# A four-layer graph network on one core: the block order of hop 2 and of layer 3, kept blocks counted from resident masks, and row 0 of each mask through GpSimd's queue

## The chip, the cores and the metric

The kernel runs on one core of a Trainium2 chip. The metric is the device time of one execution in microseconds (us). An execution recorded by the hardware profiler has a span (first to last instruction) besides.

## The reference, cut to what matters

Input: 3327 nodes with 64 features, `x`, and a sparse weighted matrix `adj` (3327 x 3327). Four residual layers follow each other, each with a layer norm. Layers 0 and 1 come before the part that is changed. Layer 2 has two hops, and layer 3 weights the neighbours of a node by their rank, counted from the last one, and keeps at most 100:

```python
# layer 2
for k in range(2):
    agg = adj @ x
    x = jnp.tanh(jnp.concatenate([agg, x], axis=1) @ W[k])
# layer 3
support = input @ weight
mask = (adj != 0)
rank = jnp.cumsum(mask, axis=1)
deg = rank[:, -1:]
k = jnp.minimum(deg, 100.0)
pos = rank - (deg - k)
w = mask * jnp.where(pos > 0, 0.5 ** (k - pos), 0.0)
out = w @ support + bias
# after each layer
x = layernorm(x + layer(x))
```

## The kernel before, in words

**Tiling.** The matrix is passed in transposed and padded to 3328. It is cut into 26 blocks of 128 rows (the neighbours j) by 3328 columns (the nodes i); a block in f32 is 1664 KB. The 3328 columns are two halves of 1664, and a half is four chunks of 416. `slot` gives the place of a block's features.

**Buffers.** Seven blocks stay in SBUF: 25 to 22 (`kept`, loaded at the start) and 20, 21, 19 (tile `late`). The rest is streamed through five buffers: four in pool `strm` (loads named `at_l`) and one in pool `more` (`bt_l`). `block` (L214) issues a load on SyncE's queue; the load waits until the last user of its buffer is done.

**Layer 2.** Each hop (loop `k`, L490) adds block after block into PSUM: `add` (L512) is two matmuls (the two halves of the columns, 64 output rows each) for a chunk, sixteen for a block, on line 515. `top` and `bottom` (L500, L505) bring in the weights, `chunk_end` (L615) adds the blocks in `end` and does the tanh. Hop 1 takes the four blocks loaded early, then kept blocks with three streamed ones after each. Its last five streamed blocks (14 to 18) are still in their buffers when hop 2 starts and are hop 2's `ready`.

**Counts for layer 3.** Layer 3 needs for each block the number of neighbours that come after it. `t_masks` (L439) makes 0/1 masks in bf16 of a block on VectorE, one for each half, into the buffers `tm` and `over`; `t_counts` (L448) adds them up on TensorE (line 452, eight matmuls a block) into `t_ps`. In hop 1 this starts with the ninth block of the order, for kept and streamed blocks alike; kept blocks not counted by the end of the loop (25, 21, 19) are counted around the hop's end (L624 to L631). The first seven streamed blocks (0 to 6) are counted in hop 2. When all 26 are counted, `t_out` (L459) writes them to `t_rows` in DRAM by GpSimd's queue.

**Resident masks.** In hop 2, `both_masks` (L360) writes a whole block's mask (128 x 3328 bf16, VectorE) into `over` or into a half of the memory of a kept block that hop 2 has used already (`slots_of`). The dictionary `place` says after which step of the order which block is masked into which place. In this kernel the masks of the seven kept blocks and of the streamed blocks 17 and 18 end up resident: nine of the 26.

**Layer 3.** `steps` lists 52 pairs (half, block). Those whose mask isn't resident, 34 of them, are loaded again as half blocks of 832 KB (`load`, tile `ah`, four buffers) and masked by `masks(q)` (six buffers, L369). Row 0 of each mask is not the mask's first row but the count of the blocks after it: it is fetched from `t_rows` by a small DMA. In this kernel `masks` puts the step on a list, and `first_row` (L351), called at the head of the next step, issues the DMA on ScalarE's queue. For a resident mask GpSimd's queue does it once for both halves (L614).

For each step q and each of two column groups c: `count` (L643) multiplies a triangle with the mask into PSUM (line 646), `read` (L651) turns the counts into weights (ScalarE, or VectorE for c = 1 in odd steps), and `products` (L843) multiplies them with the features. The high parts are multiplied at once (line 851), the low parts once in seven steps (line 868, 28 matmuls). The loop at L1021 holds the order: `read(·, q)`, one entry of `with_step`, at most one `masks` of the list `to_mask` (as long as fewer than six mask buffers are held), `products(q - 3, ·)` and `count(·, q + 1)` through `advance`. PSUM for the counts is one tile for each c, so the count of step q + 1 waits for the read of step q. The list `with_step` splits the features of the parts B, C, E of the blocks in steps 3 to 9: a copy on ScalarE, then a subtraction on GpSimd (`other_parts`, L779). The entry of step 9 also calls `first_rows` (L876), sixteen small DMAs on GpSimd's queue into `sf`, which `first_products` (L889) multiplies. `firsts_weighted`, in step 6, is three operations of VectorE.

**What sets the order.** In these layers the order on TensorE and GpSimd, and on VectorE and ScalarE, is that of the program text (`manual_schedule`). A queue runs its entries one after the other: what stands behind a waiting instruction waits too. The DMAs of SyncE's queue are issued as their buffers come free.

Of the kernel before, what the change touches and what calls it, by code (L numbers as in the profile page):

```python
# [21 lines left out]
NB = 26  # L22
# [3 lines left out]
HALF = NP // 2  # L26
NBH = NB // 2
# [17 lines left out]
FIRST_T = 8  # L45
BATCH_T = 2
# [35 lines left out]
def kernel(  # L82
# [11 lines left out]
    nc = tc.nc  # L94
# [42 lines left out]
    kept = {}  # L137
# [67 lines left out]
    for h in range(2):  # L205
        rows, last = slice(h * D, (h + 1) * D), slice((h + 1) * D - 1, (h + 1) * D)
# [106 lines left out]
    def layers(ctx, x2, x3, begun_here, kept, ready, ahead_ctx, strm):  # L313
# [9 lines left out]
        over = carry.tile([P, NP], BF16, name="over")  # L323
        t_rows = dram.tile([NB + 1, NP], BF16, name="t_rows")
# [7 lines left out]
        in_order.enter_context(  # L332
            tc.manual_schedule(engines={mybir.EngineType.PE, mybir.EngineType.Pool})
        )
        steps = [(h, jb) for h in range(2) for jb in range(NB - 1, -1, -1)]
        mask, ws = {}, {}

        ahead, to_load = {}, []
# [7 lines left out]
                    ahead[q], adjT[jb * P : (jb + 1) * P, h * HALF : (h + 1) * HALF]  # L346
                )

        no_row = []

        def first_row(keep):  # L351
            while len(no_row) > keep:
                q = no_row.pop(0)
                h, jb = steps[q]
                half = slice(h * HALF, (h + 1) * HALF)
                nc.scalar.dma_start(mask[q][:1, :], t_rows[jb + 1 : jb + 2, half])

        resident = {}

        def both_masks(jb, at):  # L360

            nc.vector.tensor_scalar(at, blocks[jb], 0.0, None, ALU.not_equal)  # L362
            resident[jb] = at

        def slots_of(jb):
            at = kept[jb].bitcast(BF16)
            return at[:, :NP], at[:, NP:]

        def masks(q):  # L369
            h, jb = steps[q]  # L370
            mask[q] = l3m.tile([P, HALF], BF16, tag="mask", name=f"mask_{h}_{jb}")
            nc.vector.tensor_scalar(mask[q], ahead.pop(q), 0.0, None, ALU.not_equal)  # L372
            no_row.append(q)
            load()

        groups = fours
# [52 lines left out]

            return rows.rearrange("b (h c k) -> c b h k", h=2, c=CPH)  # L430

        t_done, t_made, t_begun, t_ps = set(), [], set(), []

        def halves_of(t):
            return [t[:, h * HALF : (h + 1) * HALF] for h in range(2)]
# [3 lines left out]
        def t_masks(jb):  # L439

            t_done.add(jb)
            for h, of in enumerate(halves_of(blocks[jb])):
                m = t_at.pop(0)
                t_at.append(m)
                nc.vector.tensor_scalar(m, of, 0.0, None, ALU.not_equal)  # L445
                t_made.append((jb, h, m))
# [36 lines left out]
        with tc.tile_pool(  # L483
# [6 lines left out]
            for k in range(2):  # L490
# [36 lines left out]
                order = list(ready)  # L527
                if k:
                    end = [jb for jb in kept if jb not in soon]
                    for i, jb in enumerate(soon):  # L530
                        order.insert(2 * i + 1, jb)
                    order += others
                    place = {
                        0: [(soon[0], over)],
                        1: list(zip(soon[1:3], slots_of(soon[0]))),
                        3: list(zip((soon[3], end[0]), slots_of(soon[1]))),
                        6: [(order[6], slots_of(soon[2])[0])],
                        7: list(zip(end[1:], slots_of(soon[3]))),
                        8: [(order[8], slots_of(soon[2])[1])],
                    }  # L540
# [45 lines left out]
                for i, jb in enumerate(order):  # L586
                    if jb not in blocks:
                        if len(seen) % (UNDER_WAY + MORE) < MORE :
                            blocks[jb] = held[jb] = block(more, jb, tag="bt", name=f"bt_l2_{k}_{jb}")
                        else:  # L590
                            blocks[jb] = block(strm, jb, tag="at", name=f"at_l2_{k}_{jb}")
                        seen[jb] = blocks[jb]
                    if i or not k:
                        for c in range(CPH):
                            add(c, jb)
                    if jb not in t_done and (k or i >= FIRST_T):
                        t_masks(jb)
                        if len(t_made) == len(t_at) or len(t_done) == NB:
                            t_counts()
                    if k:  # L600
                        for b, at in place.get(i, ()):
                            both_masks(b, at)
                    if k == 0 and begun_here:

                        if i == 8:
                            for c in range(CPH):
                                bottom(c)

                            warm_t = small.tile([P, 1], F32, tag="warm", name="warm_t")
                            nc.scalar.activation(warm_t, hT[:, :1], AF.Tanh)  # L610
                    if k and i == 8 + len(t_left):
                        t_out()
                        for b, at in resident.items():
                            nc.gpsimd.dma_start(at[:1, :], t_rows[b + 1 : b + 2, :])  # L614
                def chunk_end(c):  # L615
                    for jb in end:
                        add(c, jb, jb == end[-1])
# [2 lines left out]
                if k:  # L620
                    break
                t_counts()
                t_left = [jb for jb in order if jb not in t_done and jb not in kept]
                last_t = [jb for jb in kept if jb not in t_done]  # L624
                for i, jb in enumerate(last_t):
                    t_masks(jb)
                    if i % BATCH_T == BATCH_T - 1 and jb != last_t[-1]:
                        t_counts()
                for c in range(CPH):
                    chunk_end(c)  # L630
                t_counts()  # L631

                last = sorted(list(seen)[-UNDER_WAY - MORE :], key=lambda jb: jb not in held)
                ready = {jb: seen[jb] for jb in last}
# [44 lines left out]
        more_ctx.close()  # L679
        l3m = ctx.enter_context(tc.tile_pool(name="l3m", bufs=MASKS, reuse_waits="tile"))  # L680
        m0 = first_masks()
        for q, (h, jb) in enumerate(steps):
            if jb in resident:
                mask[q] = resident[jb][:, h * HALF : (h + 1) * HALF]
# [157 lines left out]

        def products(q, c):  # L843
            h, jb = steps[q]
            first, last = jb == NB - 1, jb == 0
            if first:
                acc[h, c] = acc_tile(f"acc3_{h}_{c}")[:, :, :CW]

            def high(q, c):
                for e in range(2):  # L850
                    nc.tensor.matmul(  # L851
                        acc[h, c][:, e, :], s12[:, slot(jb)].rearrange("p t d -> p (t d)"),
                        ws[q, c][:, e, :], start=first, stop=last,
                    )
# [1181 lines left out]
```

## Time and profile before

| what | value |
|---|---|
| time, three runs | 559.77, 560.41, 561.75 us (median 560.41) |
| the profiled execution | 558.62 us; its span 556.9 us |
| TensorE clock granted | 0.987 |
| busy over the span | TensorE 91%, VectorE 73%, ScalarE 53%, GpSimd 41% |
| hop 1 of layer 2 | first matmul at 237.0 us, last block at 324 us |
| hop 2 | from 325 us to 423 us |
| layer 3, loop over 52 steps | from about 430 us to 543 us |

How it is read: a line of a timeline has the start, the length, the engine, the source line, what is written from what, how many instructions were merged, and in brackets the idle time ahead and what ended it. A line of waits has who waited, for whom, the total in us, how often, and the longest. A line of the DMA view ends with the size in KB and the median time from issue to landing. `PE` is TensorE, `DVE` VectorE, `ACT` ScalarE, `POOL` GpSimd, `SPq` SyncE's queue. The tile `cnt` on line 515 is the memory of hop sums, which layer 3 uses for its counts. `x2` and the like are numbers of instructions in a line.

### The profile page before, as it was taken

The numbers are of one execution on the slowest core, as the hardware profiler recorded it, in microseconds if no ns is written. First come the engines' busy times: TensorE is split into PE (matmuls) and PEld (weight loads), VectorE is DVE, ScalarE is ACT, GpSimd is POOL, SyncE is SP. The second block draws the span as 40 slices with busy tenths as digits, with TensorE's granted clock in tenths as the row PEclk, the third lists the DMA queues.
The fourth block names the chain that finished last, engine by engine and source line by source line (L and its number), as shares of the span: only waits on it lengthen the run. The fifth ranks groups of instructions, "written<-read, shape, count | busy, mean of one in ns | idle before, by whom it ended". The sixth has DMA issues, their size and how long they took to land. (4 is left out here: it accounts for less than half of the span.)

```text
span 556.9 us, 7703 instructions
## 1 busy us (share of the span) xinstructions
PE 509.1 (91%) x2865; PEld 209.5 (38%) x2865; DVE 404.1 (73%) x577; ACT 293.6 (53%) x345; POOL 229.6 (41%) x121
## 2 busy tenths in 40 slices
PE   8889999999999999999999899899788789989892
PEld 5522222222222223944333344333234344454442
DVE  6899999999999999898555616653027976456513
ACT  4899999999999996600000010000016756566541
POOL 4599999999999996000000000001410270000000
PEclk9999999999999999899999999999999999999997
DMA  8978776676777454999996007699961799907501
GB/s 298 346 227 291 238 241 225 213 241 203 234 241 226 142 217 152 376 423 425 425 427 257 1 0 261 245 416 421 386 232 44 242 390 402 388 1 233 231 1 36
DMA packets 34138, 139.20 MB, mean 250 GB/s; under 512 B 11199, under 2 KB 12977, under 8 KB 28971
## 3 DMA queue, kind: packets, MB, share of 16 engines
q1 hardware_dynamic: 30503, 137.29, 66.9%
q10 hardware_dynamic: 2404, 0.70, 0.6%
q0 software_dynamic: 1184, 0.63, 0.5%
q8 instruction: 24, 0.39, 0.3%
q14 instruction: 23, 0.19, 0.1%
HBM read 136.93 MB, written 1.04 MB: 248 GB/s over the span
## 5 line engine op out<-in xcount | busy, mean ns | idle before, releaser
L1251 POOL TENSOR_TENSOR sg<-sg,at 128x1664 f32<-128x1664 f32 x44 | 163.5, 3742 | 1.3 <-ACT sg L1239 1.2
L1279 ACT ACTIVATE pq<-pq,al,ga 128x832 f32<-128x832 f32 x104 | 104.7, 1012 | 10.9 <-DVE a L1278 10.9
L1266 PE MATMUL pq<-riT,ljT 64*128 64x416 f32 x416 | 100.8, 561 | 10.3 <-DVE v L1287 6.2
L1287 DVE SCALAR_TENSOR_TENSOR v<-pq,a 128x832 f32<-128x832 f32 x104 | 105.4, 1014 | 3.2 <-ACT pq L1279 2.2
L1278 DVE SCALAR_TENSOR_TENSOR a<-pq,sg 128x832 f32<-128x832 f32 x104 | 105.2, 1012 | 0.5 <-PE prep_fours L1357 0.4
L515 PE MATMUL cnt<-at_l,lj 128*64 128x416 f32 x496 | 91.4, 515 | 4.3 <-DMA at_l<-in_adjT 4.3
L1296 PE MATMUL acc<-v,xv 128*64 128x416 f32 x416 | 95.3, 537 | 0.0
L1239 ACT ACTIVATE sg<-lb,rb 128x1664 f32<-128x1664 f32 (+1 forms) x53 | 87.2, 1648 | 0.0
L618 ACT ACTIVATE x<-cnt 128x416 f32<-128x416 f32 x8 | 4.1, 517 | 155.8 <-PE cnt L515 155.8
L661 ACT ACTIVATE w<-cnt 128x832 int16<-128x832 f32 x79 | 65.9, 864 | 36.9 <-PE cnt L646 24.2
L464 POOL DMA_DIRECT2D t_rows<-tb x4 | 2.6, 711 | 146.7 <-DVE tb L462 146.7
L1266 PEld LDWEIGHTS pq<-riT,ljT 64*128 64x128 f32 x416 | 31.3, 184 | 83.7 <-DVE v L1287 82.9
L515 PEld LDWEIGHTS cnt<-at_l,lj 128*64 128x64 f32 x496 | 34.3, 137 | 55.7 <-issue 48.1
L851 PE MATMUL acc<-w,s 128*128 128x416 bf16 x208 | 52.4, 339 | 1.3 <-DVE sq L755 0.5
L1296 PEld LDWEIGHTS acc<-v,xv 128*64 128x64 f32 x416 | 20.6, 134 | 61.8 <-issue 58.0
L372 DVE TENSOR_SCALAR mask<-ah 128x1664 bf16<-128x1664 f32 x34 | 35.5, 1057 | 11.0 <-DMA ah<-in_adjT 6.5
L515 PE MATMUL cnt<-kept,lj 128*64 128x416 f32 x224 | 41.7, 515 | 0.4 <-DVE lj L503 0.4
L659 DVE TENSOR_SCALAR w<-cnt 128x832 int16<-128x832 f32 x25 | 25.5, 1020 | 20.3 <-PE cnt L646 20.3
L646 PE MATMUL cnt<-mask,tri 128*128 128x416 bf16 x136 | 35.0, 338 | 5.4 <-DVE w L659 2.8
L646 PEld LDWEIGHTS <-tri 128*128 128x128 bf16 x208 | 19.7, 97 | 36.3 <-issue 21.6
L1251 POOL TENSOR_TENSOR sg<-sg,kept 128x1664 f32<-128x1664 f32 (+1 forms) x10 | 30.0, 3019 | 0.0
L445 DVE TENSOR_SCALAR tm<-at_l 128x1664 bf16<-128x1664 f32 x16 | 15.7, 1023 | 16.8 <-PE t L452 16.8
(317 smaller groups left out, 468.5 us busy)
## 6 DMA issues: line engine op xcount, KB each, us to landing
at_l<-in_adjT SPq DMA_DIRECT2D x27, 1664.0 KB
at<-in_adjT SPq DMA_DIRECT2D x44, 832.0 KB
ah<-in_adjT SPq DMA_DIRECT2D x34, 832.0 KB
kept<-in_adjT SPq DMA_DIRECT2D x7, 1664.0 KB
bt_l<-in_adjT SPq DMA_DIRECT2D x6, 1664.0 KB
lb<-lf_rows SPq DMA_DIRECT2D x2, 384.0 KB
mask<-t_rows ACTq DMA_DIRECT2D x34, 3.2 KB
ljT<-ljT SPq DMA_DIRECT2D x4, 128.0 KB
```

What stands on the lines that cost most here:

```text
L372: nc.vector.tensor_scalar(mask[q], ahead.pop(q), 0.0, None, ALU.not_equal)
L515: nc.tensor.matmul(acc[c][h * D : (h + 1) * D, :], hw[:, slot(jb), :], blocks[jb][:, o : o + CW], start=c not in begun, stop=last, skip_gr ...
L646: nc.tensor.matmul(cnt[c][:, e, :], tri, mask[q][:, of], start=True, stop=True, skip_group_check=True,)
L661: nc.scalar.activation(w.bitcast(I16), cnt[c], AF.Relu)
L851: nc.tensor.matmul(acc[h, c][:, e, :], s12[:, slot(jb)].rearrange("p t d -> p (t d)"), ws[q, c][:, e, :], start=first, stop=last,)
L1239: nc.scalar.activation(sg[:, :, of], lbs[:, :, of], AF.Sigmoid, bias=rb[:, sl : sl + 1])
L1251: nc.gpsimd.tensor_tensor(sg[:, :, of], sg[:, :, of], at[:, :, of], ALU.mult)
L1266: nc.tensor.matmul(pq[:, h, :], ljT[h != jb // NBH][rows, of], riT[rows, ch * CW : (ch + 1) * CW], start=True, stop=True,)
L1278: stt(a_s[t], pqs[t], CUBIC_PLUS, us.pop(t), op0=ALU.add, op1=ALU.mult)
L1279: nc.scalar.activation(pqs[t], pqs[t], AF.Square, bias=al[:, one], scale=ga[:, one])
L1287: stt(w, pqs.pop(t), CUBIC_REST, a_s.pop(t), op0=ALU.add, op1=ALU.mult)
L1296: nc.tensor.matmul(accs[cp, ci][h * D : (h + 1) * D, :], xv[:, slot(jb), :], w[:, h, :], start=(jb == orders[cp][0]), stop=(jb == orders[c ...
```

## The change

- **Hop 1** counts only streamed blocks (from the ninth of the order on): 7 to 18. No kept block is counted there.
- **Hop 2** takes its order as 14, 15, 16, 17, 18 (what hop 1 left), then 25, 24, 23, 22, then the streamed blocks 0 to 13. Before, the kept blocks 25 to 22 stood between the first five.
- **Resident masks** are now of the seven kept blocks and of 12 and 13, the last two streamed ones. `both_masks` puts a kept block on the list of what is to be counted, and `t_counts` counts it from the resident mask in hop 2. `t_out` comes when all are counted; the rows of 12 and 13 are fetched after the loop.
- **Layer 3's steps** are mixed. For the first half: 25, 24, 23, 22, 10, 11, 7, 8, 20, 9, 4, 5, 21, 6, 17, 18, 0, 19, 1, 2, 3, 12, 14, 15, 16, 13; for the second: 10, 11, 25, 7, 8, 24, 9, 4, 23, 5, 6, 22, 17, 18, 20, 0, 1, 21, 2, 3, 19, 14, 15, 12, 16, 13. Before, a half ran from 25 down to 0, the resident nine first.
- **Row 0** of a loaded mask is fetched by GpSimd's queue, in `masks` itself.

```diff
-        steps = [(h, jb) for h in range(2) for jb in range(NB - 1, -1, -1)]
+        steps = []
...
-        def first_row(keep):
-            while len(no_row) > keep:
-                q = no_row.pop(0)
-                h, jb = steps[q]
-                half = slice(h * HALF, (h + 1) * HALF)
-                nc.scalar.dma_start(mask[q][:1, :], t_rows[jb + 1 : jb + 2, half])
...
             nc.vector.tensor_scalar(at, blocks[jb], 0.0, None, ALU.not_equal)
             resident[jb] = at
+            if jb not in t_done:
+                t_done.add(jb)
+                t_made.extend((jb, h, m) for h, m in enumerate(halves_of(at)))
...
             nc.vector.tensor_scalar(mask[q], ahead.pop(q), 0.0, None, ALU.not_equal)
-            no_row.append(q)
+            half = slice(h * HALF, (h + 1) * HALF)
+            nc.gpsimd.dma_start(mask[q][:1, :], t_rows[jb + 1 : jb + 2, half])
             load()
...
+        def rows_of(jbs):
+            for jb in jbs:
+                nc.gpsimd.dma_start(resident[jb][:1, :], t_rows[jb + 1 : jb + 2, :])
...
-                    for i, jb in enumerate(soon):
-                        order.insert(2 * i + 1, jb)
-                    order += others
+                    r = len(order)
+                    order += soon + others
                     place = {
-                        0: [(soon[0], over)],
-                        1: list(zip(soon[1:3], slots_of(soon[0]))),
-                        3: list(zip((soon[3], end[0]), slots_of(soon[1]))),
-                        6: [(order[6], slots_of(soon[2])[0])],
-                        7: list(zip(end[1:], slots_of(soon[3]))),
-                        8: [(order[8], slots_of(soon[2])[1])],
+                        1: [(soon[0], over)],
+                        r: list(zip(soon[1:3], slots_of(soon[0]))),
+                        r + 1: list(zip((soon[3], end[0]), slots_of(soon[1]))),
+                        r + 3: list(zip(end[1:], slots_of(soon[3]))),
                     }
+                    for i, at in zip((-2, -1), slots_of(soon[2])):
+                        place[len(order) + i] = [(order[i], at)]
...
-                    if jb not in t_done and (k or i >= FIRST_T):
+                    if k and len(t_made) > 2 * BATCH_T:
+                        t_counts()
+                    if jb not in t_done and jb not in kept and (k or i >= FIRST_T):
                         t_masks(jb)
-                        if len(t_made) == len(t_at) or len(t_done) == NB:
+                        if len(t_made) >= len(t_at):
                             t_counts()
...
-                    if k and i == 8 + len(t_left):
+                    if k and len(t_done) == NB and not t_ends:
+                        t_ends.append(i)
+                        t_counts()
                         t_out()
-                        for b, at in resident.items():
-                            nc.gpsimd.dma_start(at[:1, :], t_rows[b + 1 : b + 2, :])
+                        rows_of(resident)
+                if k:
+                    rows_of(order[-2:])
...
-                last_t = [jb for jb in kept if jb not in t_done]
-                for i, jb in enumerate(last_t):
-                    t_masks(jb)
-                    if i % BATCH_T == BATCH_T - 1 and jb != last_t[-1]:
-                        t_counts()
                 for c in range(CPH):
                     chunk_end(c)
-                t_counts()
...
+        here = list(resident)
+        rest = [jb for jb in range(NB) if jb not in resident]
+        rest.sort(key=lambda jb: next(i for i, g in enumerate((10, 7, 4, 0)) if jb % NBH >= g))
+        for h in range(2):
+            n = len(here) - (4 if h == 0 else 0)
+            mixed = here[:-n]
+            late_here = here[-n:]
+            for i, jb in enumerate(rest):
+                mixed.append(jb)
+                while late_here and (i + 1) * n >= (n - len(late_here) + 1) * len(rest):
+                    mixed.append(late_here.pop(0))
+            steps += [(h, jb) for jb in mixed]
...
-            first, last = jb == NB - 1, jb == 0
+            first, last = q % NB == 0, q % NB == NB - 1
...
-            if c and jb == 6:
+            if c and q % NB == NB - 4:
                 first_products(h)
...
-            first_row(1 if to_mask else 0)
```

More of the change, by code (lines that the diff above doesn't have):

```diff
@@ L347, in load @@
                 )
-        no_row = []
-        def first_row(keep):
-            while len(no_row) > keep:
-                q = no_row.pop(0)
-                h, jb = steps[q]
-                half = slice(h * HALF, (h + 1) * HALF)
-                nc.scalar.dma_start(mask[q][:1, :], t_rows[jb + 1 : jb + 2, half])
         resident = {}
@@ L430, in by_chunk @@
             return rows.rearrange("b (h c k) -> c b h k", h=2, c=CPH)
-        t_done, t_made, t_begun, t_ps = set(), [], set(), []
+        t_done, t_made, t_begun, t_ps, t_ends = set(), [], set(), [], []
+        def rows_of(jbs):
+            for jb in jbs:
+                nc.gpsimd.dma_start(resident[jb][:1, :], t_rows[jb + 1 : jb + 2, :])
         def halves_of(t):
@@ L622, in layers @@
                 t_counts()
-                t_left = [jb for jb in order if jb not in t_done and jb not in kept]
-                last_t = [jb for jb in kept if jb not in t_done]
-                for i, jb in enumerate(last_t):
-                    t_masks(jb)
-                    if i % BATCH_T == BATCH_T - 1 and jb != last_t[-1]:
-                        t_counts()
                 for c in range(CPH):
                     chunk_end(c)
-                t_counts()
                 last = sorted(list(seen)[-UNDER_WAY - MORE :], key=lambda jb: jb not in held)
```

## The prediction

> **What bounds the kernel now.** I read the timelines of TensorE, SyncE's queue, GpSimd and VectorE from 230 us on, then the waits and the DMA view. The change leaves everything before hop 1 of layer 2 (237 us) alone. Hop 1 is bound by TensorE. It has no gap until its last blocks are counted, which VectorE's masks hold up:
>
> ```profile
> 314.49 0.53 PE L452 MATMUL t<-over,upto 128*32 128x416 bf16 x8
> 315.62 0.36 PE L452 MATMUL t<-tm,upto 128*32 128x416 bf16 x4 [0.60 <-DVE tm L445]
> ...
> 318.43 0.36 PE L452 MATMUL t<-over,upto 128*32 128x416 bf16 x4 [0.57 <-DVE over L445]
> 318.72 5.81 PE L515 MATMUL cnt<-kept,lj 128*64 128x416 f32 x32
> 324.45 0.54 PE L452 MATMUL t<-tm,upto 128*32 128x416 bf16 x8
> ```
>
> From 314.94 to 318.72 TensorE does only two kept blocks' counts (3.8 us), and a third block costs 0.47 us at 324.45. Hop 2 then ends in a DMA limit, with gaps ahead of each block:
>
> ```profile
> 401.44 3.01 PE L515 MATMUL cnt<-at_l,lj 128*64 128x416 f32 x16 [1.24 <-DMA at_l<-in_adjT]
> 406.34 3.01 PE L515 MATMUL cnt<-at_l,lj 128*64 128x416 f32 x16 [1.89 <-DMA at_l<-in_adjT]
> ```
>
> SyncE's queue says when its last stretch of loads began: block 4 at 360.12, block 5 at 361.99, and from there the DMA engines are full until 402.
>
> ```profile
> 360.12 0.33 SPq L216 DMA_DIRECT2D at_l<-in_adjT  x1
> ```
>
> Layer 3 (430 to 543 us) is a loop in which a mask, its count, its read and its product follow each other. Its waits from 422 us on:
>
> ```profile
> ACT w L661 <- DVE mask L372: 11.9, 7, 2.8
> DVE w L659 <- PE cnt L646: 20.3, 15, 5.1
> ...
> DVE mask L372 <- DMA ah<-in_adjT: 6.5, 5, 2.4
> ```
>
> VectorE waits for a load; its reads, in line behind, come late; and ScalarE, whose queue issues row 0, waits for the mask. VectorE's reads (every second step) are 3.16 us apart when nothing is late, 5.74 us with a batch of 28 L868 matmuls (2.58 us).
>
> GpSimd's queue is what the change loads. It holds this burst (L876 `first_rows`), beside VectorE's masks:
>
> ```profile
> 444.43 1.16 POOL L782 TENSOR_TENSOR s<-sq,s 128x512 bf16<-128x512 f32 x1 [5.12 <-ACT s L781]
> 445.53 1.04 POOL L883 DMA_DIRECT2D sf<-s  x1
> 446.56 0.54 POOL L887 DMA_DIRECT2D sf<-s  x1
> ...
> 452.32 1.30 POOL L883 DMA_DIRECT2D sf<-s  x1 [1.81 <-DMA sf<-s]
> ...
> 457.81 0.51 POOL L887 DMA_DIRECT2D sf<-s  x1
> ```
>
> ```profile
> m<-in_adjT POOLq DMA_DIRECT2D x4, 84.5 KB, 2.3
> t_rows<-tb POOLq DMA_DIRECT2D x4, 43.9 KB, 8.0
> kept<-t_rows POOLq DMA_DIRECT2D x8, 6.5 KB, 7.7
> sf<-s POOLq DMA_DIRECT2D x8, 1.6 KB, 5.5
> ```
>
> The last column is the landing time: 2.3 us with the DMA engines nearly idle, 5.5 to 8.0 us when they are full.
>
> **What the Trainium skill says.** (1) "DMA: Bandwidth & Descriptors", section "Anatomy of one DMA — SWDGE (gpsimd) path": a GpSimd DMA has a fixed part of about 2.0 us, mostly the receipt of the write. The 2.3 us above agrees. (2) "SBUF — State Buffer", section "SBUF: two separate sides": a VectorE instruction in a two-port mode locks GpSimd out, so that it can't write descriptors. The trace agrees: the sf issues take 0.50 to 0.54 us, but 0.94 to 1.30 us (five of them) each time a mask (444.95, 447.89, 452.49, 454.58, 456.70) runs beside; ScalarE's row issues took 0.22 us throughout. (3) Same DMA page, section "Queues, rings and completion order": the DMA engines take turns between queues. The 5.5 us landings under load show that this doesn't make a small transfer quick here.
>
> **The change, part by part.** The sum is against the profiled execution: span 556.9, 1.7 around it, 558.6 us. The median of the runs shown is 560.41, 1.8 more; I add the change to the median.
>
> *Counts leave hop 1.* Four kept blocks leave the stream (two batches of 0.81 us: 1.6), two the stalled stretch (3.8), one 324.45 (0.5): hop 2 starts 5.9 us earlier, its block 15 at 328.9 instead of 334.75. Hop 1's loads have room: they are over at 303.
>
> *Hop 2's order.* Blocks 15 to 18, 25, 24, 23, 22 take 8 x 2.79 us, to 351.2. The counts of 25, 24, 23 (0.41 each) wait for VectorE: masks of 24 and 23 start with 25's end at 342.9 and take 2 x 1.89 us; with the counts 1.5 us, so 352.7. Then masks 21 and 19 (3.8) and block 0's two (1.96) on VectorE, to 358.5. That frees the buffer of block 5. Blocks 0 to 4, whose buffers come free from 328 on, have landed by then (five at 4.0 us at 425 GB/s), so nine blocks remain, where in the kernel before ten remained at 360.12. Ten took 46.2 us until block 13 could be used; nine take 41.6, to 400.1; the stream ends at 403.0 instead of 409.2: **-6.2**. TensorE alone would be there at 399 (from 358.9: six blocks with counts at 3.41, seven at 2.8), so the moved counts (7 x 0.41 and the waits) are hidden by loads; uncovered they cost up to 4 us. No more is gained, since four loads can't make up for the buffer that stands idle from 350 to 358. Against TensorE's end the bound is -10; with more straggling it is -4. The 21.5 us from the stream's end to the first VectorE read of the loop (430.69) keep their order: the loop starts at 424.5.
>
> *Mixing.* In the kernel before steps 9 to 25 and 35 to 51 are loads in a row, at 2.0 us each. The intervals of VectorE's reads show the excess: 0.9, 1.0 (449.37 to 457.64), 0.8, 1.0 (466.59 to 475.14), 0.8, 1.6 (519.87 to 528.57), together **-6.1** when loads alternate with resident blocks and ScalarE no longer waits for row issues.
>
> *What the mixing takes away.* The loop makes one mask per step from step 3 on. Before, the first loaded block stood at step 9, so each mask was some five steps early. Now it is step 4, whose mask is made in step 3, the step that counts it. The lead is 0 for steps 4 to 7, 1 for 9 to 11, 2 for 13 to 16, 3 from 18 on. A count waits for the mask (1.02) and then row 0 from GpSimd (0.2 to issue, 2.4 to 3.2 to landing: I take 2.4 where no load has just been issued, 3.2 beside one; bounds 2.0 and 5.5), and everything on TensorE, ScalarE and VectorE behind it waits. The chain, read 3 ending at 425.5:
> - Step 4: mask; GpSimd's split of part B before it in its queue ends 427.4; row issued 427.6, lands 430.6. Counts and reads of 4, then 5: VectorE's read 5 at 433.4. It was 434.54; so of the 6 us gained **4.9 are lost**.
> - Steps 6, 7: rest of C (0.5) and mask 6 to 435.9, row 439.4. Reads of 6 on ScalarE to 441.6; only then its copy for part C, GpSimd's split to 443.8, and behind it row 7 (lands 446.3). Read 7 at 447.5, was 440.61: **8.0 lost** more.
> - Step 9: mask 9 to 449.5, row 452.7, read 9 at 453.9, was 444.01: **3.0**.
> - Step 11: the split of E, then 16 sf issues stand ahead of row 11. Now few masks run beside: 16 x 0.51 + 2 x 0.55 = 9.3 us (before 12.8 with the wait of 1.8). Split ends 456.1, burst 465.4, row lands 467.9, read 11 at 469.1, was 449.37: **9.8**.
> - Steps 14, 16: lead of 2 steps (3.2 us) against 1.0 + 0.2 + 3.2: about 1 us each, **2.0**.
>
> Sum of what is lost: 27.7. ScalarE gains 34 x 0.22 us of issues, off the path here. Second half: lead 5, no loss. Net -6.2 - 6.1 + 27.7 = +15.4: 574.0 for the profiled execution, **576** on the median.
>
> **Rivals.**
> - *The burst is covered* (GpSimd's 16 issues find slack after the stalls ahead of them, costing 1 us instead of 9.8): +6.6, **567**. For it: it cost nothing before. Against it: in the changed program's order on GpSimd, step 11's row stands behind all sixteen, and its lead is one step.
> - *Rows land as under load* (5.5 us): 2.3 to 3.1 more at the five rows on the chain, 13.1; it needs loads in flight all the time: +28.5, **589**. Against it: loads now pause with the stalls.
> - *Rows land in time; faster.* One mechanism: the row's chain of mask, issue and landing fits in the time that TensorE has other counts for. Then only the two gains stand: -12.3, **548**. It decides when the row waits of steps 4 to 16 together fall under 12.3 us. Against it: at 2.0 us of landing and 8.2 us of burst they are still about 21; it would need a mask further ahead than the loop makes it.
> - *Little of it shows*: row waits of about 12, no change, **560**.
>
> **How the numbers follow.** Forecast 576 (570 to 582): 0.57; burst covered, 567 (563 to 570): 0.18; loaded landing, 589 (582 to 595): 0.14; faster 0.07; no change 0.04. Range 563 to 588 leaves out the last two and half of the loaded case: 0.18. It takes in the bounds (rows at 2.0 us and a stream end at 399: about 565). Within 0.3% (1.7 us) is what a measurement can't tell from no change. Faster 0.07, same 0.04, slower 0.89.
>
> **What would show it.** Right: hop 2 starts near 329, its stream ends near 403; TensorE idle in the steps 4 to 11 of layer 3, some 25 us in all, the longest piece (9 to 12 us) ahead of the count of block 5 and behind the sf burst on GpSimd; no VectorE wait for loads after 475. Wrong: read 11 before 460, or a TensorE without gaps from 430 to 460; or a stream end near 409, which would say that hop 1's counts came back in hop 2.

## The result and the profile after

| | before | after |
|---|---|---|
| time, median of 4 runs each on one chip (us) | 561.08 (559.77 to 562.93) | 591.07 (588.91 to 593.10) |
| ratio, 95% interval | | 1.0531 [1.0482, 1.0581] |
| profiled execution, its span | 558.62, 556.9 | 588.91, 587.1 |
| TensorE clock granted | 0.987 | 0.957 |

The change costs 30 us. The forecast was 576 with a range to 588: the side was right, the size about half of what came.

The pages of both kernels show where. Their second part has TensorE's busy tenths and its granted clock in 40 slices of the span. First the kernel before (13.9 us a slice):

```profile
PE   8889999999999999999999899899788789989892
PEclk9999999999999999899999999999999999999997
```

Then the changed kernel (14.7 us a slice):

```profile
PE   8889999999999998999999999998725449898993
PEclk9999999999999999999999999999965878999997
```

In the 30th to the 33rd slice of the changed kernel (426 to 484 us) TensorE is at 2 to 5 tenths, and in the same place its clock falls to 5 to 8 tenths. In the kernel before, neither is there.

The hops did what was forecast. TensorE's timeline of the changed kernel, at the start and the end of hop 2:

```profile
328.46 11.39 PE L514 MATMUL cnt<-at_l,lj 128*64 128x416 f32 x64
...
399.36 3.01 PE L514 MATMUL cnt<-at_l,lj 128*64 128x416 f32 x16 [1.71 <-DMA at_l<-in_adjT]
402.21 4.36 PE L514 MATMUL cnt<-kept,lj 128*64 128x416 f32 x24
```

Block 15 starts at 328.46 (forecast 328.9), the last blocks still wait for their loads (1.71), and the stream ends at 402.2 (forecast 403.0). VectorE's first read in the loop is at 423.73; before it was at 430.69.

Layer 3 then loses 37 us. The waits of the changed kernel from 420 us on (total, times, longest), and the counts that waited for row 0 on TensorE's timeline:

```profile
ACT w L657 <- PE cnt L642: 73.6, 38, 9.7
...
POOL mask L368 <- DVE mask L366: 37.0, 9, 9.1
PE cnt L642 <- DMA mask<-t_rows: 36.1, 9, 9.3
```

```profile
430.54 1.54 PE L642 MATMUL cnt<-mask,tri 128*128 128x416 bf16 x4 [6.05 <-DMA mask<-t_rows]
442.29 0.85 PE L642 MATMUL cnt<-mask,tri 128*128 128x416 bf16 x2 [7.47 <-DMA mask<-t_rows]
448.66 0.85 PE L642 MATMUL cnt<-mask,tri 128*128 128x416 bf16 x2 [3.44 <-DMA mask<-t_rows]
458.51 0.85 PE L642 MATMUL cnt<-mask,tri 128*128 128x416 bf16 x2 [4.14 <-DMA mask<-t_rows]
474.85 0.85 PE L642 MATMUL cnt<-mask,tri 128*128 128x416 bf16 x2 [9.35 <-DMA mask<-t_rows]
484.74 0.51 PE L642 MATMUL cnt<-mask,tri 128*128 128x416 bf16 x2 [3.65 <-DMA mask<-t_rows]
```

These are the counts of steps 4, 6, 7, 9, 11 and 14, six of the seven places that the forecast named (step 16 has no such wait; the three waits not shown, in later steps, are 2.0 us together). Steps 4 to 11 make 30.5 us of it, where the forecast had some 25. TensorE waits 36.1 us for rows in all; ScalarE and VectorE wait for the counts, not for a cause of their own. The bracket shows only the idle piece just ahead of an instruction: the 9.35 us of step 11 is what is left of a chain that began with the sf burst, and for that one reads GpSimd's timeline:

```profile
426.40 1.04 POOL L368 DMA_DIRECT2D mask<-t_rows  x1
437.29 0.49 POOL L368 DMA_DIRECT2D mask<-t_rows  x1 [9.13 <-DVE mask L366]
...
446.77 0.52 POOL L368 DMA_DIRECT2D mask<-t_rows  x1
453.26 1.34 POOL L368 DMA_DIRECT2D mask<-t_rows  x1 [5.98 <-DVE mask L366]
...
461.95 1.03 POOL L891 DMA_DIRECT2D sf<-s  x1
...
473.01 1.00 POOL L368 DMA_DIRECT2D mask<-t_rows  x2
```

Row 11 stands behind the burst (461.95 to 473.01). And from the start of an issue to the count that follows it: row 4 426.40 to 430.54, 4.1 us; row 6 5.0; row 9 5.2; row 14 (issued at 480.27) 4.5; but row 7 1.9 and row 11 1.8. SyncE's queue tells the two kinds apart. It issued a load at 425.72, 437.03 and 452.99, just ahead of rows 4, 6 and 9: the mask that a row belongs to is also what frees the load's buffer. Rows 7 and 11 had been held up behind GpSimd's other work, and so no longer stood beside a load that had just begun.

Last, the clock. A table by stretches of 5 us of the changed kernel (busy time and number of instructions of TensorE, its weight loads, VectorE, ScalarE, GpSimd; then the granted clock, the DMA engines' busy share, GB/s):

```profile
440.00:445.00 5.00, 2.71 (x8) 1.02 (x8) 0.13 (x1) 1.30 (x2) 0.00 (x0) 0.50 0.66 221
445.00:450.00 5.00, 1.56 (x5) 0.58 (x5) 0.00 (x0) 1.28 (x3) 1.38 (x2) 0.50 0.00 1
450.00:455.00 5.00, 4.37 (x13) 1.62 (x11) 3.50 (x4) 2.65 (x4) 1.34 (x1) 0.56 0.22 52
...
470.00:475.00 5.00, 0.15 (x1) 0.14 (x2) 0.00 (x0) 0.00 (x0) 3.55 (x8) 0.50 0.06 10
475.00:480.00 5.00, 5.00 (x20) 2.27 (x19) 2.80 (x4) 2.31 (x3) 0.00 (x0) 0.67 0.00 0
480.00:485.00 5.00, 1.35 (x8) 0.60 (x7) 3.59 (x4) 0.94 (x2) 2.01 (x4) 1.00 0.84 291
```

After the wait of 7.47 us the clock is 0.50 and stays there through the next wait. While it is at half, a group of two counts or products starts 0.69 us after the one ahead of it, in place of 0.35 (the mean of the counts from loaded masks is 377 ns, before 338). Dense matmuls bring the clock back: from 475 to 480 TensorE is busy all the time at a mean of 0.67, and then the clock is 1.00. "TensorE: Matmul & The Clock Gate", section "What's actually happening", states just this: half rate after an idle window of about 3.4 us, full rate after about as long a busy one. The trace agrees (with those two states, a mean of 0.67 over 5 us is 3.3 us at half rate), and the forecast, which listed idle pieces of 9 to 12 us, did not price it.

### The profile page after: what moved, and what is told of

It reads as the page before. It is cut to its first block, busy times and chain, and to the rows that moved or that the text cites. A ratio compares the mean times of both kernels' runs of the same rounds, so it can differ in the third digit from the quotient of the medians.

```text
span 587.1 us, 7670 instructions
## 1 busy us (share of the span) xinstructions
PE 516.2 (88%) x2865; PEld 210.3 (36%) x2865; DVE 389.6 (66%) x563; ACT 293.8 (50%) x345; POOL 246.8 (42%) x155
## 5 line engine op out<-in xcount | busy, mean ns | idle before, releaser
L642 PE MATMUL cnt<-mask,tri 128*128 128x416 bf16 x136 | 39.3, 377 | 37.4 <-DMA mask<-t_rows 36.1
L859 PE MATMUL acc<-w,s 128*128 128x416 bf16 x208 | 57.8, 367 | 1.3 <-DVE sq L763 0.5
L368 POOL DMA_DIRECT2D mask<-t_rows x34 | 18.4, 541 | 79.2 <-DVE mask L366 37.0
L444 DVE TENSOR_SCALAR tm<-at_l 128x1664 bf16<-128x1664 f32 x20 | 19.6, 1022 | 25.5 <-PE t L451 25.4
## 6 DMA issues: line engine op xcount, KB each, us to landing
at_l<-in_adjT SPq DMA_DIRECT2D x27, 1664.0 KB, 11.9
```

Source lines behind the costliest of these rows:

```text
L642: nc.tensor.matmul(cnt[c][:, e, :], tri, mask[q][:, of], start=True, stop=True, skip_group_check=True,)
L859: nc.tensor.matmul(acc[h, c][:, e, :], s12[:, slot(jb)].rearrange("p t d -> p (t d)"), ws[q, c][:, e, :], start=first, stop=last,)
```

## The experiments

*Theory*: the loss is the prediction's chain (a mask made in the step that counts it, row 0 behind it on GpSimd's queue), with terms mis-sized: a slower landing, a halved clock, a longer burst. *Rival 1*: rows by GpSimd's queue are the cost, wherever the loaded steps stand. *Rival 2*: the hops or the mixed order lose by themselves. Each ratio is against the kernel before on the same chip. Line numbers in the edits' traces shift by a few.

| kernel | median us | ratio, 95% interval |
|---|---|---|
| the change | 591.07 | 1.0531 [1.0482, 1.0581] |
| hops alone | 555.01 | 0.9872 [0.9836, 0.9907] |
| eight residents first | 564.62 | 1.0054 [1.0033, 1.0075] |
| eight first, burst in four | 555.25 | 0.9888 [0.9849, 0.9927] |
| eight first, ScalarE rows at once | 568.64 | 1.0132 [1.0069, 1.0196] |
| nine first, second half mixed, ScalarE rows a step later | 554.56 | 0.9886 [0.9851, 0.9922] |
| kernel before with GpSimd rows | 569.34 | 1.0151 [1.0103, 1.0199] |
| the change, ScalarE rows at once | 584.01 | 1.0422 [1.0329, 1.0515] |
| the change, sf on SyncE's queue | 588.45 | 1.0492 [1.0444, 1.0541] |
| the change, burst in four | 588.05 | 1.0480 [1.0408, 1.0552] |
| the change without most loads | 578.66 | 1.0317 [1.0247, 1.0388] |
| the change, short fill | 601.54 | 1.0700 [1.0658, 1.0742] |
| the change, long fill | 586.02 | 1.0431 [1.0361, 1.0502] |

**Hops alone.** The nine resident steps come first in both halves, and rows go by ScalarE's queue one step later, as before.

```diff
-            nc.gpsimd.dma_start(mask[q][:1, :], t_rows[jb + 1 : jb + 2, half])
+            no_row.append(q)
...
-            mixed = here[:-n]
-            late_here = here[-n:]
+            mixed, late_here = list(here), []
...
+            first_row(1 if to_mask else 0)
```

> One part alone: the changed hops and resident masks, but layer 3 takes the nine resident blocks first in both halves, and row 0 goes through ScalarE's queue one step late, as before. If the loss is all in layer 3 (my theory: masks without lead, rows waited for), this kernel is faster than before by what hop 2's end gained, 6 to 7 us (552 to 554 in the profiled execution). If the new order of the hops costs something later (masks of blocks 12 and 13, rows of the resident masks late), it is at or above 558.

It took 555.01, some 2 us above what was expected, and 1.3% under the kernel before. Rival 2 falls for the hops: they are a gain of some 7 us. What is lost, 36 us against this kernel, is lost by the steps' order and the rows' queue.

**Eight residents first.** The lead is lengthened and nothing else is changed.

```diff
-            n = len(here) - (4 if h == 0 else 0)
+            n = len(here) - (8 if h == 0 else 0)
```

> One number changed in the changed kernel: eight resident blocks instead of four ahead of the first loaded one in the first half, so that the first mask is made five steps before its count. Lead theory: the stalls at steps 4 to 9 vanish; only the sixteen sf issues still hold one row for some 5 us; 553 to 558, no slower than before. Rival, that rows through GpSimd's queue are slow as such, with lead or without: still 575 or more. Rival, that the drop of TensorE's clock is the cause and not the result: the clock stays low and the time stays over 570.

One number takes 26 us away: 564.62. All row waits of steps 4 to 9 are gone, so the short lead was their cause, and rival 1 falls as the main one. It is not as fast as expected. TensorE's timeline of this kernel has one long row wait left (a second has 1.74 us):

```profile
457.93 0.87 PE L642 MATMUL cnt<-mask,tri 128*128 128x416 bf16 x2 [8.88 <-DMA mask<-t_rows]
```

On its GpSimd the burst runs from 440.77 to 453.07, 12.3 us, and the row is issued behind it. A lead of about five steps does not cover that: VectorE's reads 13 and 15 are 13.0 us apart, in hops alone 3.3.

**Eight first, and the burst in four parts.** `first_rows` takes a list of column groups; four issues each go into steps 9, 11, 13 and 15.

```diff
-            lambda: (other_parts(E), first_rows()), lambda: x3_later(C), lambda: x3_later(E),
+            lambda: (other_parts(E), first_rows([0])), lambda: x3_later(C),
+            lambda: (x3_later(E), first_rows([1])), lambda: None,
+            lambda: first_rows([2]), lambda: None, lambda: first_rows([3]),
```

> The changed kernel with eight resident steps at the head of the first half, rows by GpSimd's queue as in the change, and the sixteen sf issues given out four at a time, in steps 9, 11, 13 and 15, instead of all in step 9. If the burst ahead of one row is what is left of the loss at a lead of eight (its wait was 8.9 us): the wait goes, 554 to 558. If rows on GpSimd are slow for another reason (locks by VectorE's masks, splits ahead of them): 560 to 565.

555.25: the 9 us went with the burst, and rows through GpSimd's queue are then no loss against hops alone (ratios 0.9888 and 0.9872, intervals overlapping). The longest row wait of TensorE is now 2.4 us.

**The kernel before with GpSimd rows.** This is the one part of the change that was thought of as harmless at a long lead.

```diff
-            no_row.append(q)
+            nc.gpsimd.dma_start(mask[q][:1, :], t_rows[jb + 1 : jb + 2, half])
```

> The kernel before, with one part of the change alone: row 0 of a loaded mask by GpSimd's queue in masks itself, not by ScalarE's queue one step later. Nine resident steps stay first, so each mask is some five steps early. If a queue's burst costs what stands behind it whatever the lead: rows behind the sixteen sf issues wait, a stall of 3 to 9 us near step 11 and a time of 564 to 570. If a lead of five steps (16 us) hides both the burst and a slow landing: no stall of TensorE for a row, ScalarE no longer waits for masks (11.9 us before), 556 to 561.

569.34, 1.5% slower. On its GpSimd the burst runs from 448.07 to 460.06, with the next rows behind it, and on its TensorE's timeline the count waits:

```profile
465.72 0.88 PE L647 MATMUL cnt<-mask,tri 128*128 128x416 bf16 x2 [7.31 <-DMA mask<-t_rows]
```

So the burst's cost (a wait of 7.3 us here, of 8.9 with eight residents first) is there with either order of the steps. At a long lead it is the part of rival 1 that stands.

**The change with sf on SyncE's queue.** The sixteen issues leave GpSimd.

```diff
-                        nc.gpsimd.dma_start(
+                        nc.sync.dma_start(
```

> The changed kernel with the sixteen small copies of first_rows on SyncE's queue instead of GpSimd's. If the row of step 11 waits because it stands behind them (my step: about 10 us), read 11 comes 9 to 13 us earlier and the time is 576 to 580. If the row would have been late anyway (the stall just moves to a landing of 4 to 5 us and the next rows), it is 582 to 588.

588.45, just above the second range: the total moved by no more than the intervals allow. Step 11's own row wait of 9.35 us is gone, and reads 9 and 11 are 6.25 us apart in place of 16.34. But SyncE needs 0.78 us for each sf issue (462.31 to 475.7), and the loads stand behind them. VectorE then waits for the load of step 16 (first line), so its mask and row are late, and the time is back in that step's count (second line):

```profile
480.31 1.03 DVE L366 TENSOR_SCALAR mask<-ah 128x1664 bf16<-128x1664 f32 x1 [7.30 <-DMA ah<-in_adjT]
486.84 0.85 PE L642 MATMUL cnt<-mask,tri 128*128 128x416 bf16 x2 [10.15 <-DMA mask<-t_rows]
```

**The change with the burst in four parts**, to see whether the terms of the sum stand beside each other at the short lead. The edit is the one shown above for the burst, without the longer lead.

> The changed kernel with one edit: the sixteen sf issues are given out four at a time, in steps 9, 11, 13 and 15, instead of all in step 9. The lead of four resident steps stays. At a lead of eight this edit was worth 9.4 us (564.62 to 555.25). If the terms of the prediction's sum stand beside each other, step 11's wait falls from 9.35 us to under 4 and the later rows are not late by more than 1 to 2 us together: 580 to 584. If the four issues ahead of each of the next rows, whose masks lead by only one to two steps, take the place of the one long wait: 585 to 590.

588.05, in the second range, and some 3 us under the change by the ratios (the intervals overlap), where the same edit gave 9.4 at the long lead. Step 11's wait fell to 2.97 us, so reads 3 to 11 take 48.2 us in place of 53.5. From 11 to 17 they take 20.4 in place of 18.3: four later rows wait 2.53, 0.50, 2.35 and 1.36 us (the last after read 17), and after the third the counts are again 0.69 us apart. The trace says why so little comes of it. Row 11 is issued 4.05 us after read 9 in place of 12.15. But it is then issued 0.6 us after a load and lands in 4.9 us; behind the whole burst, when the loads had landed, it took 1.7. So of the 8.1 us some 4.9 are left. From read 11 to read 17 the row waits are 1.2 us longer than in the change, and the mean clock is 0.84 in place of 0.88. The terms of the sum do not simply stand beside each other: while row 11 waited behind the burst, the loads landed, and without that wait it meets them.

**The change with rows by ScalarE's queue**, in `masks`, in the same step.

```diff
-            nc.gpsimd.dma_start(mask[q][:1, :], t_rows[jb + 1 : jb + 2, half])
+            nc.scalar.dma_start(mask[q][:1, :], t_rows[jb + 1 : jb + 2, half])
```

> The changed kernel with row 0 of loaded masks issued by ScalarE's queue, at once in the same step; the sixteen small copies stay on GpSimd, whose queue they now have for themselves, and loads stay on SyncE's. Lead theory: the waits of steps 4 to 9 stay (the lead is still 0), the one behind the sixteen copies (16 us from read 9 to read 11) falls to some 6: 576 to 582. Rival, GpSimd's queue is the cause of all of it (descriptors locked out by masks, splits ahead in line): waits of steps 4 to 9 go too, 560 to 568.

**The same with eight residents first.**

> Eight resident blocks ahead in the first half, and row 0 by ScalarE's queue at once. Both causes that I hold for the loss are gone (no lead, rows behind the sixteen copies), and the second half keeps its mixed order. Lead theory: 549 to 555, at or under the hops alone (555.0) by what mixing saves in the second half (up to 2.4 us). If mixing brings nothing or ScalarE's waits eat it: 555 to 558.

584.01 and 568.64, both above what was expected. The second has no row waits, and yet is no faster than with GpSimd rows. Its waits show why:

```profile
ACT w L657 <- DVE mask L366: 29.0, 14, 4.9
```

The issue waits for the mask, in ScalarE's order, and the reads behind it wait too. That wait of 29.0 us is 11.9 in the kernel before, which issues the row one step later. In the second kernel this makes reads 17 to 51 take 84.5 us, against 73.2 with GpSimd rows.

The first kernel pays the same price (84.5 us from read 17 to 51, in the change 72.9), so its small gain hides a large one: reads 3 to 17 take 52.2 us in place of 71.8, and 32.7 in the kernel before. At this short lead, then, GpSimd's queue makes about half of what is lost in steps 4 to 17. Part of that is the burst, which no longer stands ahead of row 11 (reads 9 to 11: 7.1 us in place of 16.3). Another part is the landing of the row. Here is step 4, on the timelines of ScalarE and TensorE:

```profile
428.38 0.48 ACTq L368 DMA_DIRECT2D mask<-t_rows  x1
429.94 1.54 PE L642 MATMUL cnt<-mask,tri 128*128 128x416 bf16 x4 [2.79 <-DMA mask<-t_rows]
```

The count starts 1.56 us after the row's issue (in the change 4.1), although SyncE issued a load at 428.38 too. Steps 6 and 9, the same way, have 1.55 and 1.59. In steps 5, 7 and 10, where a load had been issued 0.8 to 1.6 us ahead, it is 3.4, 3.5 and 3.0. Whether the other queue or the place ahead of the load's transfer makes the difference, no run separates.

**The change without most loads.** 30 of the 34 half-block loads are left out; the masks of their steps are made from the first four loaded tiles, so most neighbours are wrong.

```diff
+                if len(loaded) == LOADS:
+                    ahead[q] = loaded[0]
+                    loaded.append(loaded.pop(0))
+                    return
                 ahead[q] = l3w.tile([P, HALF], F32, tag="ah", bufs=LOADS, name=f"ah_{h}_{jb}")
+                loaded.append(ahead[q])
```

> The changed kernel with 30 of the 34 loads of half blocks in layer 3 left out: every mask is made from one of the first four loaded tiles, so most neighbours are wrong. Rows then land on idle DMA engines. If the landing beside a fresh load (4.1 to 5.2 us against 1.8) is the mis-sized term: waits of steps 4, 6, 9, 14 fall by 2.3 to 3.4 us each and the second half starves no more, 572 to 578. If the landing has nothing to do with loads, only the starving goes: 585 to 587.

578.66, 12 us less than the change and just above the first range. The DMA lines of the pages (KB, median us from issue to landing), the changed kernel first and then this one:

```profile
mask<-t_rows POOLq DMA_DIRECT2D x34, 3.2 KB, 5.0
```

```profile
mask<-t_rows POOLq DMA_DIRECT2D x34, 3.2 KB, 1.8
```

Nothing about the rows was changed, and they land in 1.8 us in place of 5.0. TensorE's waits in steps 4, 6, 9 and 14 are 4.53, 4.15, 2.90 and 0.19 us, 9.5 us less together. With rows on GpSimd's queue, the loads make them slow. The gain stands between reads 3 and 17 (59.2 us in place of 71.8; from 17 to 51 the two kernels take 72.7 and 72.9), where no mask of the changed kernel waits for a load either. It is not all the rows' landing: the burst has no waits for earlier DMAs here (8.9 us in place of 11.05), and the mean clock between these reads is 0.77 in place of 0.71.

**The clock.** In the first of two kernels (its edit is shown, without `fill` itself) eight extra count matmuls are put ahead of each count of a loaded block in steps 4 to 14; the real count overwrites their result. In the second, 28, 36, 16, 44 and 14 of them are put ahead of the first count alone of steps 4, 6, 9, 11 and 14.

```diff
+            if 3 <= q <= 13 and steps[q + 1][1] not in resident:
+                for _ in range(FILLS):
+                    fill(c)
             count(c, q + 1)
```

> The changed kernel with eight more count matmuls (128x416, their result is overwritten) ahead of each count of a loaded block in steps 4 to 14, which keep TensorE busy for up to 2.8 us of each wait, at the full clock; nothing is left out. If the halved clock after idle stretches costs what I read (counts and products 0.69 us apart instead of 0.35, some 6 us in all), the matmuls return part of it: 583 to 588 in spite of their own time, with a granted clock above 0.957. If the clock has no part in the loss: 590 to 600, slower by the matmuls that no wait hides.

> The changed kernel with TensorE kept busy through most of the five long row waits: 28, 36, 16, 44 and 14 more count matmuls (0.17 us each at the full clock, their result is overwritten) ahead of the first count of steps 4, 6, 9, 11 and 14; nothing is left out. The eight of the run before covered only 1.6 us of each wait, so that the clock fell all the same. If the halved clock costs about 6 us of the loss: 582 to 586, with the clock near 0.98. If what the clock does is hidden in the waits for rows: 588 to 592.

The short fill fails as an experiment: eight matmuls last 1.57 us, the waits outlast them, the clock falls all the same (0.965 mean), and much of the added work (144 matmuls) stands where no wait hides it, 601.54, above both ranges. The long fill adds nearly as many (138) and takes less time than the change, 586.02. The mean clock of its profiled execution, the slowest of the four, is 0.975; the others have 0.984 and 0.985. Its clock slices, beside those shown above:

```profile
PEclk9799999999999998999999999999997989999997
```

The ratio falls from 1.0531 to 1.0431, some 5 to 6 us. In the profiled execution reads 3 to 17 take 68.4 us in place of 71.8, 3.4 less. The two intervals overlap a little, so the size is rough, some 3 to 6 us; that more matmuls gave no slower kernel leaves little but the clock.

**Nine first, the second half mixed, rows by ScalarE a step later.**

```diff
-            nc.gpsimd.dma_start(mask[q][:1, :], t_rows[jb + 1 : jb + 2, half])
+            no_row.append(q)
...
-            mixed = here[:-n]
-            late_here = here[-n:]
+            mixed, late_here = ([], list(here)) if h else (list(here), [])
...
+            first_row(1 if to_mask else 0)
```

> The changed kernel with the nine resident steps first in the first half, mixed steps in the second half only, and row 0 by ScalarE's queue one step later, as before. If the mixing itself pays where the lead is kept (the prediction gave 0.8, 1.0, 0.8 and 1.6 us of load waits, of which those of the second half are 2.4 to 3.4): 551.5 to 553.5, under the hops-only kernel's 555.0. If loads are late as a whole and not by place: 554.5 to 556.

554.56: at the edge of the second theory's range, and no different from hops alone (0.9886 and 0.9872). The reads of both traces say the mixing in the second half is worth 0.7 us here (the last five intervals: 22.4 us, in hops alone 23.1); of the expected 2.4 to 3.4 us no more is there. In the change itself the five take 20.9 us. Three kernels (this one, hops alone, eight first with the burst in four) are 1.1 to 1.3% under the kernel before, and the runs can't rank them.

## Why the prediction was wrong in size

The reads of VectorE carry the comparison, since the prediction gave times for them. Both columns are of profiled executions; the last one is the measured interval from the read ahead less the predicted one. For 17 and 51 the prediction is the interval of the kernel before (14.06 and 74.43), less the starvation that it took away there (1.9 and 4.2), and for 17 plus the 2.0 of steps 14 and 16.

| read of step | predicted | measured | more than predicted |
|---|---|---|---|
| 3 | 424.5 | 423.73 | -0.8 |
| 5 | 433.4 | 434.58 | 1.9 |
| 7 | 447.5 | 451.01 | 2.3 |
| 9 | 453.9 | 460.86 | 3.5 |
| 11 | 469.1 | 477.20 | 1.1 |
| 17 | 14.2 later | 18.3 later | 4.2 |
| 51 | 70.2 later | 72.9 later | 2.6 |

The sum is 14.9 us, which is the gap (30.3 measured between the profiled executions, 15.4 predicted).

- **Hop 1's counts, hop 2's order: right.** -6.2 was predicted at the stream's end, -7.0 came at the first read (-4.3 to -6.8 in the other kernels with these hops, so the 0.8 us says nothing). Hop 2 stayed bound by loads, and the counts moved into it cost nothing that can be seen.
- **The chain of steps 4 to 11: right in its places, too small.** Every wait that was forecast came, in order, by the mechanism named.
- **The term that was mis-sized first is the row's landing.** 2.4 us idle and 3.2 beside a load were taken, with 5.5 as the upper bound. Measured from issue to count: 4.1, 5.0, 5.2 and 4.5 us in rows 4, 6, 9 and 14, and 1.9 and 1.8 in the two that stood beside no fresh load. For issue and landing of the four the prediction had 3.2, 3.5, 3.2 and 3.4, which is 5.6 us less together; the two others gave 1.3 back. The step that failed is the argument against the rival "rows land as under load": "loads now pause with the stalls". They pause, but each begins again at the end of the very mask whose row is then issued. The rival's own time, 589, was the nearest to what came, though only part of the excess was its mechanism. The kernel without loads is the run that shows it: its reads 3 to 17 take 59.2 us, where the prediction had 58.8 and the change took 71.8. That these two agree so closely is in part luck, since that kernel has landings of 1.8 us, shorter than predicted, and the halved clock, which the prediction left out.
- **The halved clock was no term of the sum at all.** It costs some 3 to 6 us by the long fill (5.5 in the sum below). From the table of windows, busy time times the missing share of the clock (for 440 to 445: 2.71 x 0.50) adds up to 9.9 us from 430 to 490: a ceiling, since not all of that lies on the path. The page on the clock gate would have given it in advance; a prediction that writes down idle pieces of 9 us owes it a price.
- **The burst: 9.3 predicted, 11.05 measured, 1.75 more.** It waited for earlier DMAs (2.0 us in all), as the kernel before showed once and the prediction left out.
- **The gain by mixing: too much by 2.6.** From read 17 on 4.2 us of it should have come and 1.6 did. The second half gave all of its 2.4. In the first half 1.8 was predicted, which was too much by itself: without loads reads 17 to 25 take 15.1 us, before 16.3, so only 1.2 was to be had. It lost 0.8 instead: its loads start late out of the stalls and starve again, as VectorE's timeline of the changed kernel shows, against the statement "no VectorE wait for loads after 475":

```profile
505.52 1.03 DVE L366 TENSOR_SCALAR mask<-ah 128x1664 bf16<-128x1664 f32 x1 [1.70 <-DMA ah<-in_adjT]
```

These add to 5.6 - 1.3 + 5.5 + 1.75 + 2.6 - 0.8 (the last is the earlier start of the loop), about 13.4 of the 14.9 us, or 11.3 with the 3.4 us of the long fill's trace. The parts overlap (a row that lands sooner also leaves less time for the clock to fall; without loads the clock fell too), so the runs bound them rather than split them, and 1.5 to 3.6 us have no name.

The rival "burst is covered" is refuted by the kernel before with GpSimd rows and by the pair with eight residents first; the faster case by the change itself. It would have needed a longer lead and a divided burst: both together give 0.9888.

## What to carry to other kernels

A small transfer that follows a step which also frees a big load's buffer is issued beside that load every time; price it at the landing measured under load, on the queue that will issue it, and give it a lead longer than that, counted in time. A burst of issues on one queue is a wait for whatever stands behind it, and moving the burst to another queue moves the wait: divide it where the lead is long enough (9.4 us here; at the short lead some 3), or put it where nothing behind it is due. And where a forecast has TensorE idle for several us, add the half-speed matmuls that follow.

## What the runs showed of the hardware that was not expected

- A 3.2 KB DMA of GpSimd's queue took 1.7 to 1.8 us to land with nothing beside it and 4.0 to 5.1 us when an 832 KB load had been issued 0.3 to 0.7 us earlier. "DMA: Bandwidth & Descriptors", section "Latency and other measured facts", says that the memory's latency is 0.2 us on average and up to 2 us at high load, and that this makes up most of the fixed cost; the direction agrees, the excess here (2.2 to 3.4 us) is larger.
- The same DMA from ScalarE's queue, issued in the same moment as such a load, was there for the count after 1.55 to 1.59 us, and after 3.0 to 3.5 us where a load had been issued 0.8 to 1.6 us earlier.
- An sf issue took 0.50 us on GpSimd (0.93 to 1.3 beside a mask) and 0.78 us on SyncE (start to start); a row's issue took 0.22 us on ScalarE (the first one 0.48). Sixteen of the first kind took 8.9 us without most loads, and 11.05 to 12.8 us in the changed kernel, with eight residents first and in the two kernels with the old order.
- After row waits of 4.1 to 9.4 us the granted clock was 0.50; with a few counts between the waits (440 to 450) it stayed there through a wait of 3.4. Behind the longest wait some 3.4 us of dense matmuls brought it back, behind another 2.7 us (458.51 to 461.24), and behind a third 5.7 us (448.66 to 454.37) had not.
